# A state-space scan: where one of the sixteen input scalings of two state pairs is done

## The chip, the cores and the metric

The kernel runs on one core of one Trainium2 chip. Five engines work side by side, each through its own list of instructions in order: TensorE (matrix products and transposes, in the profile PE, with its weight loads as PEld), VectorE (DVE), ScalarE (ACT), GpSimd (POOL) and SyncE (SP), whose queue starts the DMA transfers. An instruction that needs what another engine makes waits for a semaphore, and everything behind it on its engine waits too.

The metric is the device time of one execution in microseconds (us), taken as the median of several runs.

## The reference

The input is 8 images of 64 x 64 pixels with 192 channels. Two residual layers follow each other. The first (convolutions, a chunked state-space layer, two projections) is not touched by the change. The second is a two-dimensional selective scan; cut to what matters here:

```python
xs = jnp.stack([x_flat, x_t], axis=1)                              # row order, column order
xs = jnp.concatenate([xs, jnp.flip(xs, axis=-1)], axis=1)          # and both backwards: K = 4 directions
x_dbl = jnp.einsum('bkdl,kcd->bkcl', xs, x_proj_weight)            # 12 for dt, 16 for B, 16 for C
delta = jax.nn.softplus(dts + dt_projs_bias[None, :, :, None])
A = -jnp.exp(A_logs).reshape(K, D_INNER, D_STATE)                  # D_INNER = 384, D_STATE = 16

def step(hst, inp):
    d, bm, cm, uu = inp
    dA = jnp.exp(d[..., None] * A[None])
    dBu = (d * uu)[..., None] * bm[:, :, None, :]
    hst = dA * hst + dBu
    y = jnp.einsum('bkdn,bkn->bkd', hst, cm)
    return (hst, y)
```

So for every direction, each of 384 channels and each of 16 states there is a recurrence over 4096 tokens. Its decay is exp(delta * A), its input is delta * u * B, and its output is multiplied by C and summed over the 16 states. The change concerns the product (delta * u) * B.

## The kernel before, in words

The program first computes layer 0 for all images, until about 4,900 us, and then goes image by image through layer 1. In layer 1 the function `scan` builds the work of an image. Its outer loop runs over *steps*: 4 directions k times 8 stretches c of 512 tokens, so 32 steps an image and 256 in all. In directions 2 and 3 the stretches and the scans run backwards. A step has 24 *units*: 8 pairs p of states, and for each pair 3 blocks d of 128 channels. A tile of a unit holds on its 128 partitions 2 states of 64 channels; the two halves f of the block lie beside each other.

What a unit needs, and the lines that make it:

- `weigh` (L1592, ScalarE) makes `pw`. Here tokens lie on the partitions, 4 groups j of 128, and a row has the 384 channels of delta * u (`duT`). For state i of pair p the row is multiplied by that token's B, one number per partition (`bt`). The result goes into every other run of 64 columns of `pw`, so that both states of a pair stand side by side. A pair needs 4 x 2 = 8 such scalings, two pairs sixteen. They serve all three units of the pair.
- `supply` (L1618, TensorE) turns `pw` by 8 transposes of 128 x 128 into `g` in PSUM: channels and states on the partitions, 512 tokens along the row.
- `decay` (L1607, ScalarE) makes `ea` = exp(delta * A) from `dr`, two instructions.
- `run` (L1634, VectorE) does the two scans `hs` = ea * state + g, starting from `cy`, the last state of the step before (a direction's first step starts from zero). GpSimd then copies the last column into `cy` (L1646) and multiplies `hs` by C into `hc` (L1648).
- `collect` (L1663, TensorE) sums the two states of `hc` into `y` in PSUM, over all pairs. In direction 0 and for p = 0 a product for the skip connection (L1661) stands ahead of it.
- `add` (L1672, L1674, VectorE) adds the finished `y` of the three blocks to `yacc`.

The order of all this is written out by hand in `main`; no planner changes it. Behind the scans of unit u are issued: `decay` of unit u + 2, then three, three or two `weigh` for d = 0, 1, 2 (they are taken from one list, `todo`, ten ahead), `supply` of unit u + 1, `collect` of unit u - 1, `add` of unit u - 2, and last the pieces that prepare the next step. Those pieces (`prepare`) stand at fixed units: the projection p_d on TensorE behind units 2, 3 and 4 (L1481), its copy `xdbl` on VectorE behind 5 (L1488), `bt` on VectorE behind 7 (L1504), p_dt on TensorE behind 7, 9 and 12 (L1510), the softplus on ScalarE behind 8, 10 and 13 (L1517, L1518), `de` on VectorE behind 9, 11 and 14 (L1523), its transpose p_du on TensorE behind 11, 14 and 16 (L1532), and `duT` on VectorE behind 12, 15 and 17 (L1539). Here a unit's number in its step is 3p + d, and a piece "behind" a unit stands in the lists after what `main` issues for that unit. All loads go through SP's queue.

Buffers: three of `ea`, three each of `hs` and `hc`, two of `g`, eight of `pw` (two pairs). `scan` is entered for each image after a stretch in which the image before is finished and the new one is prepared.

Of the kernel before, what the change touches and what calls it, by code (L numbers as in the profile page):

```python
# [9 lines left out]
AF = mybir.ActivationFunctionType  # L10
# [18 lines left out]
NB1 = TT // 128  # L29
# [1003 lines left out]
def layer1(tc, consts, x1s, mv1, out, w_in, w_x, w_dt, w_out):  # L1033
    nc = tc.nc
# [6 lines left out]
    with ExitStack() as ctx:  # L1041
# [49 lines left out]
        o = lambda ins: keeper[-1](ins)  # L1091
# [343 lines left out]
        def scan(xo):  # L1435
# [149 lines left out]
            def weigh(s, p, j, i):  # L1585

                st = state[s]
                if i == 0:
                    st["pw", p, j] = pools["pw1"].tile([128, 2 * DT, 2, 64], F32, name="pw")
                n = 2 * p + i  # L1590
                o(
                    nc.scalar.activation(  # L1592
                        st["pw", p, j][:, :, i],
                        st["duT"][:, j].rearrange("p (g c) -> p g c", c=64),
                        AF.Copy,
                        scale=st["bt"][:, j, n : n + 1],
                    )
                )

            def decay(u):  # L1600
                s, p, d = units[u]
# [79 lines left out]
            def prologue(f, mq, front_pools):  # L1681

                yield "wait", "front"
                front_pools.close()
                for name, n in (("pr1", 2), ("dr1", 4), ("pw1", 8), ("bc1", 3), ("e1", 3)):
                    spool(name, n)
                load_first = prepare(0, lambda name: mq.tile([128, TT], F32, name=name, tag="mm"))
                ready.update({fn.__name__: fn for at in sorted(load_first) for fn, *_ in load_first[at]})
                r = yield step("SP", 0.1, ready["load"])
                yield "take", "mm"  # L1690
                r += 3.5
                for d in range(DT):
                    r = yield step("PE", 0.95, lambda: ready["project"](d), r)
                r = yield step("DVE", 0.7, ready["keep"])
                f.give("mm", r)
                f.at["xd"] = r
                yield "take", "mm"
                yield step("PE", 0.6, ready["turn_b"])
                r = yield step("DVE", 0.2, ready["keep_b"])
                f.give("mm", r)  # L1700
                f.at["bt"] = r
                load_c(0, 0)
                for d in range(DT):
                    yield "wait", ("du", d)
                for t in todo[:10]:
                    yield step("ACT", 0.55, lambda: weigh(*t), f.free["ACT"])
                for u in range(2):
                    yield step("ACT", 1.35, lambda: decay(u), None, "explog")
# [19 lines left out]
            def main():  # L1728
                for name, n, kw in (("h1", 3, {}), ("y1", 1, dict(space=PSUM)), ("g1", 2, dict(space=PSUM))):
                    spool(name, n, **kw)  # L1730
                supply(0)
                rest = iter(todo[10:])
                nu = len(units)
                for u, (s, p, d) in enumerate(units):
                    if p == 0 and d == 0:
                        pieces = prepare(s + 1) if s + 1 < len(steps) else {}
                    s2, p2 = (s, p + 1) if p < NP1 - 1 else (s + 1, 0)
                    if s2 < len(steps) and d == 0:
                        load_c(s2, p2)
                    run(u)  # L1740
                    if u + 2 < nu:
                        decay(u + 2)
                    for _ in range((3, 3, 2)[d]):
                        if t := next(rest, None):
                            weigh(*t)
                    if u + 1 < nu:
                        supply(u + 1)
                    if u >= 1:
                        collect(u - 1)
                    if u >= 2:  # L1750
                        add(u - 2)
                    for f, *args in pieces.get(p * DT + d, ()):
                        f(*args)
                collect(nu - 1)
                add(nu - 2)
                add(nu - 1)
                cx.close()
# [136 lines left out]
```

## Time and profile before

| what | value |
|---|---|
| median of 3 runs | 23751.5 us (23744.67 to 23764.05) |
| the profiled execution | 23759.13 us, its span 23757.4 us |
| busy: PE, DVE, ACT, POOL | 21089.6, 21274.2, 21040.0, 16067.4 us |
| scalings `pw`, ScalarE, L1592 | 16384, mean 601 ns |
| decays `ea`, ScalarE, L1607 | 12288, mean 709 ns |
| scans `hs`, VectorE, L1634 | 10752 of mean 1262 ns and 1536 of 1202 ns |
| products `hc`, GpSimd, L1648 | 6144, mean 2375 ns |
| one ordinary step (9142.23 to 9207.80 us) | 65.57 us |

In a row of the groups, the line, the engine and the operation are followed by what is written and read, the number of instructions, their busy time and the mean of one. After the last bar stands the time that the engine was idle just before them, and what ended it. The durations of successive instructions of VectorE and ScalarE overlap by some tens of nanoseconds, so what an instruction costs its engine is rather the distance to the start of the next. In a timeline each row is a start, a duration, an instruction or several equal ones in a row, and in brackets the idle time before it with what ended that.

### The profile page before, as it was taken

To read this page: it belongs to the slowest core of one execution; us is meant where nothing else is said; L and a number is where in the kernel's file an instruction comes from. 1 tells how busy PE (TensorE), PEld (TensorE's weight loads), DVE (VectorE), ACT (ScalarE), POOL (GpSimd) and SP (SyncE) were. 2 spreads that over 40 slices of the span, in tenths; PEclk is the share of its full clock that TensorE was granted. 3 is DMA by queue.
4 is the path that set the end of the run, shared out by engine and by line. 5 is a ranking of instruction groups with operands and counts; after the bars stand their busy time and mean duration, and the time that the engine had idled before them with its cause. 6 is when DMAs were issued, how large, how long until landed. Compare 5 with 4: busy or idle time off the path is not lost.

```text
span 23757.4 us, 313126 instructions
## 1 busy us (share of the span) xinstructions
PE 21089.6 (89%) x100804; PEld 10279.5 (43%) x100804; DVE 21274.2 (90%) x22093; ACT 21040.0 (89%) x37507; POOL 16067.4 (68%) x12871
## 2 busy tenths in 40 slices
PE   7999999978888888888888888888888888888888
PEld 4444444434444444444444444444444444444444
DVE  7888888779998999899989998999899989998998
ACT  5666766669998999899989998999899989998998
POOL 1111111149995999599959985998699769976997
PEclk8999999989999999999999999999999999999999
DMA  2111111133233323333233233323332233233332
GB/s 50 45 44 44 46 44 43 39 99 81 81 79 107 81 82 78 107 81 82 76 112 81 82 77 109 81 81 79 110 82 81 78 107 82 81 85 100 82 83 67
DMA packets 1368290, 1859.75 MB, mean 78 GB/s; under 512 B 268576, under 2 KB 697024, under 8 KB 1357440
## 3 DMA queue, kind: packets, MB, share of 16 engines
q1 hardware_dynamic: 1366656, 1839.73, 28.7%
q8 instruction: 810, 13.27, 0.2%
q14 instruction: 824, 6.75, 0.1%
HBM read 1225.98 MB, written 210.50 MB: 60 GB/s over the span
## 4 chain that ended last, share of the span: by engine, by line
POOL 43%; PE 24%; ACT 15%; DVE 7%; issue 6%; DMA 4%; SPq 1%; POOLq 0%; ACTq 0%; DVEq 0%
POOL hc L1648 40%; ACT pw L1592 6%; ACT ea L1607 6%; POOL cy L1646 3%; PE p_f L956 3%; DMA xc<-xo 2%; DVE xs L1202 2%; PE p_f L976 2%; PE p_x L448 2%; PE y L1663 2%; PE p_o L873 2%; PE p_y L790 1%; PE g L1618 1%; PE p_d L1481 1%; PE p_z L531 1%
## 5 line engine op out<-in xcount | busy, mean ns | idle before, releaser
L1648 POOL TENSOR_TENSOR hc<-hs,cb 128x1024 f32<-128x1024 f32 x6144 | 14592.9, 2375 | 12.0 <-POOL cy L1646 9.9
L1634 DVE TENSOR_TENSOR_SCAN hs<-ea,cy,g 128x512 f32<-128x512 f32 x10752 | 13024.0, 1262 | 608.6 <-PE g L1618 411.1
L1592 ACT ACTIVATE pw<-duT,bt 128x384 f32<-128x384 f32 x16384 | 8874.1, 601 | 20.2 <-DVE duT L1539 20.2
L1607 ACT ACTIVATE ea<-dr,an 128x512 f32<-128x512 f32 x12288 | 8120.5, 709 | 189.2 <-DVE hs L1634 170.8
L1663 PE MATMUL y<-hc,sel 128*64 128x512 f32 x24576 | 6624.0, 617 | 1841.3 <-POOL hc L1648 1819.2
L1618 PEld LDWEIGHTS g<-ident,pw 128*128 128x128 f32 x49152 | 5288.7, 141 | 4336.8 <-issue 2671.4
L1618 PE MATMUL g<-ident,pw 128*128 128x128 f32 x49152 | 6788.4, 279 | 60.1 <-ACT pw L1592 28.6
L1646 POOL COPY cy<-hs 128x2 f32<-128x2 f32 x6144 | 1164.2, 189 | 3373.5 <-DMA out_x<-xl 1733.8
L1663 PEld LDWEIGHTS y<-hc,sel 128*64 128x64 f32 x24576 | 1225.9, 134 | 3254.1 <-POOL hc L1648 3031.3
L1634 DVE TENSOR_TENSOR_SCAN hs<-ea,g 128x512 f32<-128x512 f32 x1536 | 1763.7, 1202 | 159.0 <-PE g L1618 115.6
L365 POOL TENSOR_TENSOR s<-xs 96x512 f32<-96x512 f32 x64 | 121.1, 1892 | 2033.7 <-DVE xs L343 1522.9
L1202 DVE SCALAR_TENSOR_TENSOR xs<-pad,p,xs 128x4096 f32<-128x4096 f32 x192 | 860.9, 4484 | 43.4 <-ACT xs L1192 36.2
L1510 PE MATMUL p_dt<-xdbl,wd 13*128 13x512 f32 x1536 | 857.2, 639 | 41.0 <-DVE de L1523 39.1
L365 POOL TENSOR_TENSOR s<-sq 96x512 f32<-96x512 f32 x128 | 211.6, 1653 | 964.1 <-ACT sq L378 899.8
L1481 PE MATMUL p_d<-xc,wx 128*44 128x512 f32 x1536 | 791.6, 598 | 22.6 <-DMA xc<-xo 22.0
L343 DVE SCALAR_TENSOR_TENSOR x<-xx,p,x 96x512 f32<-96x512 f32 x1024 | 785.2, 815 | 19.4 <-ACT x L332 19.4
L956 PE MATMUL p_f<-h,wf 96*128 96x512 f32 x1536 | 761.9, 632 | 24.4 <-ACT zs L550 14.0
L343 DVE SCALAR_TENSOR_TENSOR xs<-xin,p,xs 96x512 f32<-96x512 f32 x1024 | 749.3, 767 | 4.6 <-ACT xs L332 4.6
L976 PE MATMUL p_f<-m,wf 128*96 128x512 f32 x1536 | 692.9, 601 | 0.0
L1532 PEld LDWEIGHTS p_du<-ident,de 128*128 128x128 f32 x3072 | 323.5, 141 | 610.2 <-DVE de L1523 405.8
L448 PE MATMUL p_x<-h,wi 96*128 96x512 f32 x1024 | 544.5, 664 | 12.3 <-ACT h L405 11.1
L365 POOL TENSOR_TENSOR s<-x 96x512 f32<-96x512 f32 x64 | 96.2, 1502 | 626.3 <-DVE x L343 477.2
(202 smaller groups left out, 19557.2 us busy)
## 6 DMA issues: line engine op xcount, KB each, us to landing
cb<-cd SPq DMA_DIRECT2D x4096, 128.0 KB
dr<-de SPq DMA_DIRECT2D x3072, 128.0 KB
xc<-xo SPq DMA_DIRECT2D x256, 768.0 KB
e<-csd SPq DMA_DIRECT2D x256, 384.0 KB
xl<-x SPq DMA_DIRECT2D x256, 384.0 KB
ut<-xo SPq DMA_DIRECT2D x128, 768.0 KB
ut<-xo SPq DMA_DIRECT2D x256, 384.0 KB
xo<-xs SPq DMA_DIRECT2D x48, 1024.0 KB
```

Source lines behind the costliest of these rows:

```text
L343: nc.vector.scalar_tensor_tensor(im(out[:, ct]), tap(ct, j), w[:, ct, j : j + 1], im(out[:, ct]), ALU.mult, ALU.add)
L956: nc.tensor.matmul(ps, wf1[:, ct, mt * 128 : mt * 128 + 128], h[:, ct], start=ct == 0, stop=ct == 1)
L976: nc.tensor.matmul(ps[:CP], wf2[:, kt, ct * CP : ct * CP + CP], m[:, kt], start=kt == 0, stop=kt == 5)
L1202: nc.vector.scalar_tensor_tensor(xs, tap(j), kw[:, d, j : j + 1], xs, ALU.mult, ALU.add)
L1481: nc.tensor.matmul(st["p_d"][:44], wx[:, d, k], st["xc"][:, d], start=d == 0, stop=d == DT - 1)
L1592: nc.scalar.activation(st["pw", p, j][:, :, i], st["duT"][:, j].rearrange("p (g c) -> p g c", c=64), AF.Copy, scale=st["bt"][:, j, n : n + 1],
L1607: nc.scalar.activation(ea[:, f], state[s]["dr", d][:, f], AF.Exp, scale=an[:, k, p, at : at + 1])
L1618: nc.tensor.transpose(g[:, f, j * 128 : j * 128 + 128], state[s]["pw", p, j][:, 2 * d + f].rearrange("p a b -> p (a b)"), ident,)
L1634: nc.vector.tensor_tensor_scan(rev(h[:, f]), rev(ea[:, f]), rev(g[:, f]), 0.0 if first(s) else state[s - 1]["cy"][:, p, d, f : f + 1], ALU ...
L1646: o(nc.gpsimd.tensor_copy(st["cy"][:, p, d], h[:, :, last]))
L1648: o(nc.gpsimd.tensor_mul(hc, h, bc(st["cb", p], 1, [128, 2, TT])))
L1663: o(nc.tensor.matmul(y[half[f]], sel, hc[:, f], start=p == 0 and k > 0, stop=p == NP1 - 1))
```

## The change

In every second pair (p odd), the eighth scaling (j = 3, i = 1) is issued to VectorE as a `tensor_scalar_mul`; the other fifteen of two pairs stay on ScalarE. It is issued at the same place in the program's text. In VectorE's list this is behind the second scan of a unit: the list `todo` runs ten ahead, so the scaling of pair p + 1 (odd) comes up in the unit with even p and d = 1, which is units 1, 7, 13 and 19 of a step. The transposes for the unit after the next are the first to read it.

```diff
                 n = 2 * p + i
-                o(
-                    nc.scalar.activation(
-                        st["pw", p, j][:, :, i],
-                        st["duT"][:, j].rearrange("p (g c) -> p g c", c=64),
-                        AF.Copy,
-                        scale=st["bt"][:, j, n : n + 1],
-                    )
-                )
+                dst, src = st["pw", p, j][:, :, i], st["duT"][:, j].rearrange("p (g c) -> p g c", c=64)
+                scale = st["bt"][:, j, n : n + 1]
+                if p % 2 and (j, i) == (NB1 - 1, 1):
+                    o(nc.vector.tensor_scalar_mul(dst, src, scale))
+                else:
+                    o(nc.scalar.activation(dst, src, AF.Copy, scale=scale))
```

## The prediction

> A step is one direction and one stretch of 512 tokens. It has 24 units, numbered here u = 3p + d (pair p = 0 to 7, column block d = 0 to 2). S(u), hc(u), y(u) and g(u) are unit u's two scans (VectorE, L1634), product with C (GpSimd, L1648), sum (TensorE, L1663) and transposed input (TensorE, L1618).
>
> **What bounds the kernel now.** First the page: engine shares, then the chain.
>
> ```profile
> PE 21089.6 (89%) x100804; PEld 10279.5 (43%) x100804; DVE 21274.2 (90%) x22093; ACT 21040.0 (89%) x37507; POOL 16067.4 (68%) x12871
> ...
> POOL 43%; PE 24%; ACT 15%; DVE 7%; issue 6%; DMA 4%; SPq 1%; POOLq 0%; ACTq 0%; DVEq 0%
> ...
> L1648 POOL TENSOR_TENSOR hc<-hs,cb 128x1024 f32<-128x1024 f32 x6144 | 14592.9, 2375 | 12.0 <-POOL cy L1646 9.9
> L1592 ACT ACTIVATE pw<-duT,bt 128x384 f32<-128x384 f32 x16384 | 8874.1, 601 | 20.2 <-DVE duT L1539 20.2
> ```
>
> ScalarE is about as busy as VectorE, yet the chain runs mostly through GpSimd and TensorE. Next one ordinary step, 9142.23 to 9207.80 us: busy time of PE, PEld, DVE, ACT and POOL after the step's 65.57 us.
>
> ```profile
> 9142.23:9207.80 65.57, 57.78 (x318) 28.49 (x316) 63.18 (x61) 65.36 (x119) 60.04 (x49) 1.00 0.33 84
> ```
>
> ScalarE has 0.2 us idle, VectorE 2.4. That looks like a ScalarE bound, so I followed the step's timelines for each VectorE wait. VectorE first (from unit 1 on), then GpSimd:
>
> ```profile
> 9139.29 2.44 DVE L1634 TENSOR_TENSOR_SCAN hs<-ea,cy,g 128x512 f32<-128x512 f32 x2
> 9141.65 0.66 DVE L1674 TENSOR_TENSOR yacc<-yacc,y 128x512 f32<-128x512 f32 x1
> ...
> 9150.41 2.45 DVE L1634 TENSOR_TENSOR_SCAN hs<-ea,cy,g 128x512 f32<-128x512 f32 x2 [0.50 <-PE g L1618]
> ...
> 9158.06 0.19 DVE L1504 COPY bt<-p_b 128x64 f32<-128x64 f32 x1
> ...
> 9161.75 2.45 DVE L1634 TENSOR_TENSOR_SCAN hs<-ea,cy,g 128x512 f32<-128x512 f32 x2 [1.14 <-PE g L1618]
> ...
> 9186.71 7.13 DVE L1634 TENSOR_TENSOR_SCAN hs<-ea,cy,g 128x512 f32<-128x512 f32 x6
> 9194.06 7.36 DVE L1634 TENSOR_TENSOR_SCAN hs<-ea,cy,g 128x512 f32<-128x512 f32 x6 [0.22 <-PE g L1618]
> ```
>
> ```profile
> 9141.80 0.19 POOL L1646 COPY cy<-hs 128x2 f32<-128x2 f32 x1 [0.39 <-DVE hs L1634]
> ...
> 9156.03 2.38 POOL L1648 TENSOR_TENSOR hc<-hs,cb 128x1024 f32<-128x1024 f32 x1
> 9158.35 0.19 POOL L1646 COPY cy<-hs 128x2 f32<-128x2 f32 x1
> ...
> 9189.39 2.38 POOL L1648 TENSOR_TENSOR hc<-hs,cb 128x1024 f32<-128x1024 f32 x1
> 9191.69 0.20 POOL L1646 COPY cy<-hs 128x2 f32<-128x2 f32 x1
> ```
>
> TensorE runs g(u+1), y(u-1), g(u+2), y(u) in that order, so S(u+3) needs g(u+3), which stands behind y(u), which needs hc(u). From the end of S(u) that is about 2.6 us to the end of hc, 1.05 for y, 1.05 for g, 0.2 to start: 5.0 us, plus 1 us where a projection (p_d, p_dt) stands between. S(9) shows it: S(6) ends at 9155.8, hc(6) at 9158.41, y(6) runs at 9158.46, p_dt 9159.47, g(9) 9160.52, S(9) at 9161.75; VectorE had 4.8 us of work in those 5.95 and idled 1.14. So each wait is explained without ScalarE, and the whole step closes the same way: S(0) to S(2) back to back; hc(2), y(2), p_d, g(5), S(5); S(6), hc(6), y(6), p_dt, g(9), S(9), S(10); hc(10), hc(11), y(11), p_dt, g(14), S(14); then VectorE without a break to S(18); hc(18), y(18), g(21), S(21); and five hc end to end, 2.45 us apart, pace S(21) to S(23). That ring is 65.57 us. ScalarE (65.36) merely fits in. In direction 0, where TensorE has six more products at p = 0, the step is 66.5 us, and the waits of one such step (7580 to 7645 us) show ScalarE itself waiting 1 us:
>
> ```profile
> ACT ea L1607 <- DVE hs L1634: 1.0, 1, 1.0
> ```
>
> Only a direction's first step (65.0 us, scans 1.12 us apart instead of 1.18) is paced by ScalarE near its end.
>
> **What the skill says.** "SBUF — State Buffer", section Who interferes with whom: a VectorE instruction in a two-port mode, or with two SBUF inputs, and a GpSimd instruction exclude each other; the first holds the port pair for its whole length. Today's scan-stage VectorE work never does that: scans, duT, de and yacc read one operand from PSUM. Layer 0 shows the exclusion (timelines of VectorE and GpSimd):
>
> ```profile
> 1380.02 1.30 DVE L761 TENSOR_TENSOR st<-st,dec 64x384 f32<-64x384 f32 x1
> 1379.64 1.27 POOL L365 TENSOR_TENSOR s<-x 96x512 f32<-96x512 f32 x1 [4.06 <-DVE x L343]
> 1380.85 0.53 POOL L436 COPY cin<-cin 128x12 f32<-128x12 f32 x1
> ```
>
> L761 (541 ns in the median) waited for the GpSimd sum, ended 0.41 us after it (384 elements streaming), and GpSimd's next instruction, 0.19 us elsewhere, waited for it: the waiting VectorE instruction went first. "VectorE: DVE Perf Modes", section on the perf-mode tier table: fp32 tensor_scalar within SBUF runs at 2×. The trace agrees (price below).
>
> **The change, part by part.** Per step, four scalings (p odd, j = 3, i = 1) move, 1024 in all.
> *ScalarE* loses 1024 starts 0.505 us apart (three take 1.52 us from start to start of what follows): 2.0 us a step, worth nothing in the ring, for it is not in it.
> *VectorE* gains 1024 tensor_scalar 128x384. Nearest rows:
>
> ```profile
> L237 DVE TENSOR_SCALAR wf<-wf,p 96x768 f32<-96x768 f32 x2 | 1.2, 610 | 4.7 <-PE p_fb L227 4.7
> L248 DVE TENSOR_SCALAR dsk<-ident,p 128x128 f32<-128x128 f32 x3 | 0.7, 270 | 0.0
> ```
>
> (610 - 270)/640 = 0.53 ns an element, two a cycle; at 384 that is 406 ns, and VectorE instructions overlap by 0.08 us (a 0.66 us yacc costs 0.58), so 0.33 us. At one a cycle: 0.6 us, 0.53 net, without exclusion. I take 0.33. Behind a running hc it ends 0.21 us (384 at 0.53) after it.
> *Order.* In the built order it stands directly behind the second scan of units 1, 7, 13 and 19, with no semaphore wait of its own; the fourth transpose of g(u+2) now waits for VectorE too. No DMA moves. Behind it queue yacc or bt and the next scan; GpSimd's cy and hc wait if it holds the ports.
> - *Unit 1*: GpSimd is idle (the 0.39), so it goes at once; it lies in the unbroken run S(0) to S(2): **+0.33**. In direction 0 the ring there is TensorE's (y, skip product, p_d end to end, S(4) and S(5) idle 0.60 and 1.29): **0**.
> - *Unit 7*: S(7) ends at 9158.14, hc(6) at 9158.41, so it waits 0.27 and runs 0.21; cover is the 1.14 us before S(9): **0**.
> - *Unit 13*: GpSimd idle; S(14) waited 0.18 for g(14) (four scans take 4.97, elsewhere 4.78), so 0.33 - 0.18 = **+0.15**.
> - *Unit 19*: S(19) ends at about 9191.5, hc(18) at 9191.77: 0.48 for VectorE against 0.22 cover at S(21); cy(19) and the five hc in a row move by 0.25: **+0.25**.
>
> So +0.73 in the 168 ordinary steps: 123 us; +0.40 in the 56 later steps of direction 0: 22 us. The 32 first steps: two groups of three units take 7.73 at ScalarE's pace, GpSimd's is 7.36, so about -0.7, less 0.33: **-0.4**, -12 us. Sum **+133 us**: 23,759.1 (span 23,757.4 and 1.7 around it) becomes 23,892. The median of the runs is 7.6 below the profiled one: 23,885.
>
> **Rivals.**
> 1. *ScalarE is the bound; faster.* For: 65.36 of 65.57 busy. Against: no scan of the step waits for ScalarE. If so, a step falls to what VectorE then needs, 63.18 + 1.32 = 64.5: -1.07 x 256 = -270, 23,480. It decides if VectorE's 2.4 idle us shrink when ScalarE is early.
> 2. *One element a cycle.* 0.53, 0, 0.35, 0.3 = 1.2 (168 steps) and 0.65 (56): +238, less 12: 23,977. For: the output has a stride between its runs of 64, which neither row has.
> 3. *The waiting scaling loses the ports to the next hc* at units 7 and 19: 2.4 us more each, 1.6 after unit 7's cover: +4 x 224 = about +1000, 24,750. Against: the 1380 us rows.
> 4. *Hidden.* The 1.4 us fit the 2.4 idle us if VectorE's lateness at units 1, 13 and 19 is caught up before the next wait: 23,750. Against: no idle time stands between S(0) and S(2).
> That the change doesn't happen is excluded by the built order.
>
> **How the numbers follow.** My case 0.52 (alone 23,835 to 23,940), rival 1 0.08, rival 2 0.16, rival 3 0.10 (partly lost ports lie between), rival 4 0.14. Dropping rival 1 and most of rival 3 leaves 23,730 to 24,100. What a measurement here can tell is about 0.2%, 48 us. Faster is rival 1: 0.08; within is rival 4: 0.14; slower is the rest: 0.78.
>
> **What would show it.** The new row: near 0.41 us on average, longer behind units 7 and 19. Ordinary step 66.3, direction 0 66.9, first steps 64.6. ScalarE idle about 2.5 us a step, waiting for hs. GpSimd's cy grows behind the scalings, hc does not. Wrong if scans wait for pw or ea before, if hc lengthens by whole microseconds, or if the row is near 0.6 us (rival 2) or 2 us (rival 3).

## The result

| | median | runs |
|---|---|---|
| before | 23757.8 us | 4 (23744.67 to 23767.62) |
| after | 23876.9 us | 4 (23864.2 to 23878.98) |

The ratio is 1.0051, 95% interval 1.0039 to 1.0063: slower by 119 us, where 133 were forecast (the sum of the steps; 23,885 for the median). The profiled execution took 23878.98 us, its span 23876.9, which is 119.5 more than the span before.

The change makes the file two lines shorter here, so L1634 is now L1632, L1618 is L1616, L1648 is L1646 and L1646 is L1644; in the kernels of the experiments a line can stand one or two off again. The decays are L1605, the scalings L1596 on ScalarE and L1594 on VectorE. The page of the changed kernel, with the lines that answer to those of before, and the row of `ea`:

```profile
PE 21014.3 (88%) x100804; PEld 10295.5 (43%) x100804; DVE 21645.8 (91%) x23117; ACT 20657.4 (87%) x36483; POOL 16193.5 (68%) x12871
...
POOL 36%; PE 25%; ACT 21%; DVE 6%; issue 5%; DMA 4%; SPq 2%; POOLq 0%; ACTq 0%; DVEq 0%
...
L1646 POOL TENSOR_TENSOR hc<-hs,cb 128x1024 f32<-128x1024 f32 x6144 | 14569.5, 2371 | 12.5 <-POOL cy L1644 11.5
...
L1605 ACT ACTIVATE ea<-dr,an 128x512 f32<-128x512 f32 x12288 | 8138.1, 710 | 645.7 <-DVE hs L1632 624.1
...
L1596 ACT ACTIVATE pw<-duT,bt 128x384 f32<-128x384 f32 x15360 | 8350.1, 601 | 21.8 <-DVE duT L1539 21.8
...
L1644 POOL COPY cy<-hs 128x2 f32<-128x2 f32 x6144 | 1269.5, 207 | 3359.5 <-DMA out_x<-xl 1745.4
```

Two of these rows in the kernel before:

```profile
L1607 ACT ACTIVATE ea<-dr,an 128x512 f32<-128x512 f32 x12288 | 8120.5, 709 | 189.2 <-DVE hs L1634 170.8
L1646 POOL COPY cy<-hs 128x2 f32<-128x2 f32 x6144 | 1164.2, 189 | 3373.5 <-DMA out_x<-xl 1733.8
```

The engines' busy times moved as the change says: ScalarE lost 383 us and VectorE gained 372. `hc` kept its length (2375 ns before). `cy` grew from 189 to 207 ns. ScalarE's waits for `hs`, in the row of `ea`, grew from 171 to 624 us. The share of ScalarE in the chain rose from 15 to 21% although it does less; the runs below show that this share is not a bound.

The new operation, from the groups with shapes kept apart:

```profile
L1594 DVE TENSOR_SCALAR pw<-duT,bt 128x384 f32<-128x384 f32 x1024 | 503.4, 492 | 0.0
```

The same ordinary step as in the prediction (9299.82 to 9366.08 us here), busy time of PE, PEld, DVE, ACT and POOL after the length, and ScalarE's waits in it:

```profile
9299.82:9366.08 66.26, 57.47 (x317) 28.51 (x318) 64.57 (x64) 63.88 (x115) 60.60 (x49) 1.00 0.32 80
```

```profile
ACT ea L1605 <- DVE hs L1632: 2.1, 4, 0.9
```

ScalarE is busy for 63.9 us of 66.3 and idle for 2.4, of which it waits 2.1 for scans: the time that it was given is spent waiting. VectorE's idle time in the step fell from 2.39 to 1.69 us, and the rest of the 1.39 us that it gained in work, 0.69 us, is what this step grew by.

The timeline of VectorE around units 19 (9282.86), 1 (9298.92) and 7 (9315.66), then GpSimd's:

```profile
9278.16 4.79 DVE L1632 TENSOR_TENSOR_SCAN hs<-ea,cy,g 128x512 f32<-128x512 f32 x4
9282.86 0.57 DVE L1594 TENSOR_SCALAR pw<-duT,bt 128x384 f32<-128x384 f32 x1
9283.35 9.77 DVE L1632 TENSOR_TENSOR_SCAN hs<-ea,cy,g 128x512 f32<-128x512 f32 x8
...
9298.92 0.40 DVE L1594 TENSOR_SCALAR pw<-duT,bt 128x384 f32<-128x384 f32 x1
9299.23 0.68 DVE L1672 TENSOR_TENSOR yacc<-yacc,y 128x512 f32<-128x512 f32 x1
...
9315.66 0.56 DVE L1594 TENSOR_SCALAR pw<-duT,bt 128x384 f32<-128x384 f32 x1
9316.13 0.21 DVE L1504 COPY bt<-p_b 128x64 f32<-128x64 f32 x1
```

```profile
9280.84 2.37 POOL L1646 TENSOR_TENSOR hc<-hs,cb 128x1024 f32<-128x1024 f32 x1
9283.16 0.31 POOL L1644 COPY cy<-hs 128x2 f32<-128x2 f32 x1
9283.43 2.37 POOL L1646 TENSOR_TENSOR hc<-hs,cb 128x1024 f32<-128x1024 f32 x1
...
9299.07 0.29 POOL L1644 COPY cy<-hs 128x2 f32<-128x2 f32 x1 [0.39 <-DVE hs L1632]
...
9313.62 2.37 POOL L1646 TENSOR_TENSOR hc<-hs,cb 128x1024 f32<-128x1024 f32 x1
9315.94 0.32 POOL L1644 COPY cy<-hs 128x2 f32<-128x2 f32 x1
```

Behind unit 1, where GpSimd is idle, the scaling takes 0.40 us, and the next instruction starts 0.31 us after it. Behind units 19 and 7 an `hc` is running. There the scaling ends 0.22 and 0.23 us after that `hc` (9283.43 against 9283.21, 9316.22 against 9315.99), and `cy` behind it takes 0.3 us in place of 0.19. In all 1024, the medians by place are 396 ns (unit 1), 559 (unit 7), 396 (unit 13) and 569 (unit 19), and 535 of them came up while an `hc` was running: all ended before the next `hc` began, 0.22 us (median) behind the running one. GpSimd is held up at the other two places as well: `cy` takes 0.29 us behind units 1 and 13, and the `hc` after it starts 0.25 us after `cy` does, in place of 0.14.

Where the time went is seen best when a step is cut where its waits end. The table has the distances between the starts of scans, from the trace, in us (0-2 is from the start of S(0) to the start of S(2), 18-0 from S(18) to S(0) of the next step): the median over 160 ordinary steps (the last step of each image is left out, since what follows it is no step).

| from S to S | 0-2 | 2-6 | 6-9 | 9-13 | 13-15 | 15-18 | 18-0 | step |
|---|---|---|---|---|---|---|---|---|
| before | 5.88 | 11.12 | 8.39 | 11.26 | 5.47 | 8.23 | 15.21 | 65.56 |
| after | 6.21 | 11.12 | 8.39 | 11.26 | 5.61 | 8.23 | 15.45 | 66.26 |
| more | 0.33 | 0 | 0 | 0 | 0.14 | 0 | 0.24 | 0.70 |

The three stretches that grew hold units 1, 13 and 19; unit 7, in 6-9, cost nothing. A later step of direction 0 grew by 0.33 (66.51 to 66.84), a direction's first step shrank by 0.52 (0.32 in direction 0). With these, 160 x 0.70 + 56 x 0.33 - 24 x 0.52 - 8 x 0.32 = 115 us of the 119.5. These are medians; the 248 steps themselves, summed, grew by 110 us.

### The profile page after: what moved, and what is told of

Its sections match the earlier page's. It is cut to its first block, busy times and chain, and to the rows that moved or that the text cites. A ratio compares the mean times of both kernels' runs of the same rounds, so it can differ in the third digit from the quotient of the medians.

```text
span 23876.9 us, 313903 instructions
## 1 busy us (share of the span) xinstructions
PE 21014.3 (88%) x100804; PEld 10295.5 (43%) x100804; DVE 21645.8 (91%) x23117; ACT 20657.4 (87%) x36483; POOL 16193.5 (68%) x12871
## 4 chain that ended last, share of the span: by engine, by line
POOL 36%; PE 25%; ACT 21%; DVE 6%; issue 5%; DMA 4%; SPq 2%; POOLq 0%; ACTq 0%; DVEq 0%
POOL hc L1646 33%; ACT pw L1596 9%; ACT ea L1605 8%; POOL cy L1644 3%; PE p_f L956 3%; PE y L1661 3%; DVE xs L1202 2%; PE p_f L976 2%; PE p_x L448 2%; PE g L1616 2%; PE p_o L873 2%; PE p_y L790 1%; DMA xc<-xo 1%; DMA dr<-de 1%; PE p_z L531 1%
## 5 line engine op out<-in xcount | busy, mean ns | idle before, releaser
L1646 POOL TENSOR_TENSOR hc<-hs,cb 128x1024 f32<-128x1024 f32 x6144 | 14569.5, 2371 | 12.5 <-POOL cy L1644 11.5
L1632 DVE TENSOR_TENSOR_SCAN hs<-ea,cy,g 128x512 f32<-128x512 f32 x10752 | 13017.5, 1262 | 404.5 <-PE g L1616 180.7
L1605 ACT ACTIVATE ea<-dr,an 128x512 f32<-128x512 f32 x12288 | 8138.1, 710 | 645.7 <-DVE hs L1632 624.1
L1596 ACT ACTIVATE pw<-duT,bt 128x384 f32<-128x384 f32 x15360 | 8350.1, 601 | 21.8 <-DVE duT L1539 21.8
L1616 PEld LDWEIGHTS g<-ident,pw 128*128 128x128 f32 x49152 | 5299.9, 141 | 4165.9 <-issue 2487.8
L1616 PE MATMUL g<-ident,pw 128*128 128x128 f32 x49152 | 6673.6, 279 | 17.6 <-DVE hs L1632 12.5
L1644 POOL COPY cy<-hs 128x2 f32<-128x2 f32 x6144 | 1269.5, 207 | 3359.5 <-DMA out_x<-xl 1745.4
L1632 DVE TENSOR_TENSOR_SCAN hs<-ea,g 128x512 f32<-128x512 f32 x1536 | 1769.1, 1202 | 103.9 <-PE g L1616 48.0
```

The lines of the kernel that those rows point to most:

```text
L1596: o(nc.scalar.activation(dst, src, AF.Copy, scale=scale))
L1605: nc.scalar.activation(ea[:, f], state[s]["dr", d][:, f], AF.Exp, scale=an[:, k, p, at : at + 1])
L1616: nc.tensor.transpose(g[:, f, j * 128 : j * 128 + 128], state[s]["pw", p, j][:, 2 * d + f].rearrange("p a b -> p (a b)"), ident,)
L1632: nc.vector.tensor_tensor_scan(rev(h[:, f]), rev(ea[:, f]), rev(g[:, f]), 0.0 if first(s) else state[s - 1]["cy"][:, p, d, f : f + 1], ALU ...
L1644: o(nc.gpsimd.tensor_copy(st["cy"][:, p, d], h[:, :, last]))
L1646: o(nc.gpsimd.tensor_mul(hc, h, bc(st["cb", p], 1, [128, 2, TT])))
```

## The experiments

The question was which of the two halves of the change costs, which of its four places, how much of it is the exclusion between VectorE and GpSimd, and whether ScalarE's gain can be had where the waits are moved.

### Each half alone

First, ScalarE's relief alone:

```diff
                 if p % 2 and (j, i) == (NB1 - 1, 1):
-                    o(nc.vector.tensor_scalar_mul(dst, src, scale))
+                    pass
...
-                                state[s]["pw", p, j][:, 2 * d + f].rearrange("p a b -> p (a b)"),
+                                state[s]["pw", p, min(j, NB1 - 2) if p % 2 else j][:, 2 * d + f].rearrange("p a b -> p (a b)"),
```

> The four scalings of a step are left out altogether (TensorE's transposes read the neighbouring block j = 2 in their place, so that share of the output is another): ScalarE is relieved exactly as by the change, VectorE gets nothing. My theory, that the step is set by a ring through VectorE, GpSimd and TensorE and not by ScalarE: ordinary step 65.56 us as before, direction 0 66.5 as before, only a direction's first step shorter, by about 0.8 us; time about 23,730 us, ratio 0.999. Rival, that ScalarE sets the step (65.36 of 65.57 us busy): the step loses between 1.1 and 2.0 us, time 23,250 to 23,480 us, ratio 0.979 to 0.989.

Then VectorE's work alone, with all sixteen scalings on ScalarE and VectorE's result put into a tile that nothing reads:

```diff
+                o(nc.scalar.activation(dst, src, AF.Copy, scale=scale))
                 if p % 2 and (j, i) == (NB1 - 1, 1):
-                    o(nc.vector.tensor_scalar_mul(dst, src, scale))
-                else:
-                    o(nc.scalar.activation(dst, src, AF.Copy, scale=scale))
+                    o(nc.vector.tensor_scalar_mul(junk, src, scale))
```

> ScalarE keeps all sixteen scalings; VectorE does the four extra ones a step at the same places into a scratch tile that nobody reads. My theory: the cost is VectorE's part alone, so ordinary step 66.26 us and direction 0 66.84 as in the changed kernel; first steps a little longer than before, since ScalarE isn't relieved; time about 23,890 us, ratio 1.006. Rival, that ScalarE's relief pays for part of VectorE's work in the changed kernel: slower than the changed kernel by up to 2 us a step, up to 24,380 us, ratio 1.026.

The relief alone gave 23686.2 us, ratio 0.9980 (0.9972 to 0.9988); VectorE's work alone 23885.4 us, 1.0063 (1.0048 to 1.0078); the kernel before took 23741.3 us on that chip. An ordinary step of the relief run, by windows, and ScalarE's waits in it:

```profile
8178.52:8244.06 65.54, 57.39 (x318) 28.52 (x316) 63.17 (x60) 63.74 (x115) 59.94 (x49) 1.00 0.31 79
```

```profile
ACT ea L1605 <- DVE hs L1632: 1.5, 3, 0.6
```

For pairs with odd p the transposes read the block j = 2 in place of j = 3 here, so TensorE waits for an earlier scaling: if anything, this kernel has less to wait for than the changed one. ScalarE is busy 1.6 us less than before, and the step has the same length: the median of all ordinary steps is 65.56 us, unchanged to 0.01 in the whole step and in each of the seven stretches. So ScalarE, at 65.36 us busy of 65.57, was not what set the pace, and rival 1 falls. The gain of the run lies in other steps: 0.16 us in direction 0, 0.92 in the first steps of the other directions and 0.67 in direction 0's (56 x 0.16 + 24 x 0.92 + 8 x 0.67 = 36 us, and 41 when the steps themselves are summed; the measured gain is 55, its interval 28 to 66). That is more than the 27 us expected: the first steps gain more, and direction 0 gains where nothing was expected.

The second run has an ordinary step of 66.26 us: 0.33, 0.14 and 0.24 more in the same three stretches, and 0 in the others. Its row is that of the changed kernel:

```profile
L1596 DVE TENSOR_SCALAR junk<-duT,bt 128x384 f32<-128x384 f32 x1024 | 505.9, 494 | 0.0
```

So in the ordinary steps the whole loss is made by VectorE's part; ScalarE's part neither adds to it nor takes from it. The output here has no stride, and the row is the same.

### Each place alone

The condition was narrowed to one pair, so that only the scaling behind unit 1 (p = 1), unit 7 (p = 3) or unit 19 (p = 7) is VectorE's:

```diff
-                if p % 2 and (j, i) == (NB1 - 1, 1):
+                if p == 3 and (j, i) == (NB1 - 1, 1):
```

> Only the scaling behind unit 1 goes to VectorE, the other three of a step stay on ScalarE. My theory: ordinary step +0.33 us, direction 0 none (TensorE's products cover it): ordinary 65.89, time about +50 us, 23,810 us. Rival, that the cost follows VectorE's time alone: a quarter of the whole, +0.18 us a step.

> Only the scaling behind unit 7 goes to VectorE. My theory: it waits for the running hc but is covered by the 1.14 us wait ahead of S(9): step unchanged (65.56), time 23,755 us within 10. Rival, a quarter of the whole: +0.18 us a step, +30 us.

> Only the scaling behind unit 19 goes to VectorE. My theory: it waits for hc(18) and then holds back cy(19) and five hc in a row: +0.24 us a step, ordinary 65.80 and direction 0 66.75, its row near 0.57 us, time about +50 us. Rival, a quarter of the whole: +0.18 us in ordinary steps and +0.08 in direction 0.

Each ran once beside one run of the kernel before (23742.7 us):

| scaling of VectorE behind | time | ordinary step, more | stretch that grew | later step of direction 0, more |
|---|---|---|---|---|
| unit 1 | 23791.1 us | 0.32 | 0-2 | -0.06 |
| unit 7 | 23706.3 us | 0 | none | -0.16 |
| unit 19 | 23764.6 us | 0.24 | 18-0 | 0.08 |

A single run says little about a few tens of us: the time before the first scan of layer 1, which none of these edits touches, runs from 5031 to 5083 us in the traces of this case. The steps, which are medians over 160, say it clearly. In an ordinary step each place costs what it costs in the full change, and the fourth, unit 13, which was not run alone, is left with 0.70 - 0.32 - 0.24 = 0.14, which is what its stretch grew by. Unit 7 alone, from the groups and from VectorE's timeline:

```profile
L1594 DVE TENSOR_SCALAR pw<-duT,bt 128x384 f32<-128x384 f32 x256 | 148.1, 579 | 0.0
```

```profile
8198.85 0.56 DVE L1594 TENSOR_SCALAR pw<-duT,bt 128x384 f32<-128x384 f32 x1
...
8202.54 2.45 DVE L1632 TENSOR_TENSOR_SCAN hs<-ea,cy,g 128x512 f32<-128x512 f32 x2 [0.64 <-PE g L1616]
```

It is the longest of the four, because `hc` is running, and it is free: the idle time before S(9), 1.14 us in the kernel before, is 0.64 here, and S(9) starts when `g` is there, as it did. With ScalarE relieved of that one scaling, this kernel is even a little faster than the one before: its 248 steps, summed, are 16 us shorter, by the steps of direction 0 (-0.16 us) and the first steps of the others (-0.34). In direction 0, unit 1 costs nothing either, as the prediction said of its ring (the closed chain of waits that sets the length of a step), which is TensorE's there: the stretch 0-2 grows by 0.33 us and 2-6 shrinks by 0.38.

### The exclusion of the ports

An operation of VectorE that takes as long but does not exclude GpSimd, at the same four places, would tell the length of the new work from the exclusion. A sum along the row was tried, into the tile that nothing reads, with all scalings on ScalarE; whether it excludes GpSimd is seen in the lengths of `cy`. Two sizes were run, 192 elements and 256:

```diff
-                    o(nc.vector.tensor_scalar_mul(dst, src, scale))
+                    o(nc.vector.reduce_sum(junk[:, 0, :1], st["duT"][:, j, :256], axis=mybir.AxisListType.X))
```

> ScalarE keeps all scalings; VectorE does a sum over 192 elements[...] at the four places, into a scratch tile, in place of the scaling of 384. If it costs about the 0.31 us of the scaling without excluding GpSimd: its row the same at all four places, cy back to 189 ns, +0.33, 0, +0.14 and only +0.1 behind unit 19: ordinary step 66.1 us against 66.26. Rival, that the longer rows behind units 7 and 19 and the 0.24 us of unit 19 have nothing to do with GpSimd: longer rows there again and 66.26 us.

> As the run with the sum over 192 elements, with 256, so that VectorE's instruction is as long as the scaling (its row near 396 ns): +0.33 behind unit 1, +0.14 behind unit 13, as the scaling. Behind unit 19 without the exclusion of GpSimd 0.33 - 0.22 = 0.1 us at most and perhaps none, with it (rival) 0.24; the row the same at all four places.

The sum of 192 took 321 to 331 ns, the sum of 256 took 385 to 394 at all four places, against 396 for the scaling where nothing hinders it. The latter, from the groups and from the timelines of VectorE and GpSimd at unit 19:

```profile
L1596 DVE TENSOR_REDUCE junk<-duT 128x1 f32<-128x256 f32 x1024 | 401.6, 392 | 0.0
```

```profile
8289.11 4.79 DVE L1632 TENSOR_TENSOR_SCAN hs<-ea,cy,g 128x512 f32<-128x512 f32 x4
8293.82 0.39 DVE L1596 TENSOR_REDUCE junk<-duT 128x1 f32<-128x256 f32 x1
8294.13 9.76 DVE L1632 TENSOR_TENSOR_SCAN hs<-ea,cy,g 128x512 f32<-128x512 f32 x8
```

```profile
8291.80 2.37 POOL L1646 TENSOR_TENSOR hc<-hs,cb 128x1024 f32<-128x1024 f32 x1
8294.11 0.19 POOL L1644 COPY cy<-hs 128x2 f32<-128x2 f32 x1
```

Here `hc` is running too (8291.80 to 8294.17), and yet VectorE starts the next scan after 0.31 us, and `cy` keeps 0.19, here and at the other three places. So what stretched the scaling from 0.40 to 0.57 us and `cy` from 0.19 to 0.31 is the exclusion, which "SBUF — State Buffer" in the Trainium skill, section Who interferes with whom, describes for two-port modes; these traces agree.

| per ordinary step, more | unit 1 | unit 7 | unit 13 | unit 19 | step |
|---|---|---|---|---|---|
| scaling (the change) | 0.33 | 0 | 0.14 | 0.24 | 0.70 |
| sum of 256, same length | 0.33 | 0 | 0.14 | 0.07 | 0.53 |
| sum of 192, shorter | 0.26 | 0 | 0.07 | 0.00 | 0.33 |

The exclusion is 0.17 us of the step's 0.70, all of it behind unit 19; the rest is plain time in VectorE's list. That `cy` is 0.1 us longer behind units 1 and 13, and the `hc` after it as much later, costs nothing: the sum, which leaves them alone, costs as much there. The lower rows also show the cover: from 0.33 us of work unit 1 pays all, unit 13 pays 0.14 and unit 19 pays 0.07. With 0.07 us less work each of the three pays 0.07 less. The kernel with the sum of 192 took 23810.2 us in one run (before: 23742.7), that with the sum of 256 took 23866.1 (before: 23762.5).

### Another order around it

Can ScalarE's gain be had in ordinary steps too, if the parts of the ring that TensorE makes are shortened? The projections p_d and the first p_dt stand on TensorE between `y` and the next `g`. In the next two kernels they are issued one place later, behind the next `g`; the copy `xdbl` then has to stand behind unit 6. One has all scalings on ScalarE, the other has the change:

```diff
-                    5: [(keep,)],
-                    6: [(turn_b,)],
+                    6: [(keep,), (turn_b,)],
...
                     if u + 1 < nu:
                         supply(u + 1)
+                    for f, *args in late:
+                        f(*args)
+                    late = []
...
                     for f, *args in pieces.get(p * DT + d, ()):
-                        f(*args)
+                        if p * DT + d < 8 and f.__name__ in ("project", "step"):
+                            late.append((f, *args))
+                        else:
+                            f(*args)
```

> The kernel before, with p_d of units 2, 3, 4 and the first p_dt put one place later in TensorE's list, behind the next unit's transposes and ahead of the next sum y (the copy xdbl moves from unit 5 to 6 with them). If these products stand in the ring between y(u) and g(u+3), VectorE's waits of 0.43, 0.50 and 1.14 us at S(4), S(5) and S(9) shrink to some 0.3 together; ring about 63.9 us, and now ScalarE's 65.36 us sets the ordinary step: -0.2 us; direction 0 about -0.9 us; time about 23,670 us, ratio 0.996. Rival, that those waits come from ScalarE or from GpSimd alone: no change, ratio 1.000.

> The changed kernel with the same move of p_d and the first p_dt as in the run before this one. My theory: with the ring shortened to about 63.9 us, the scalings on VectorE add some 1.0 (unit 7 has less cover), 64.9 us, and ScalarE needs only 63.3: 0.65 us under the ordinary step of before and 0.45 under that of the same order without the change; time about 23,590 us, ratio 0.993 to before, and here the scaling on VectorE is a gain. Rival, that VectorE's extra work costs its 0.7 us whatever the order: slower than the same order without the change by 0.5%, ratio 1.001.

| | time | ratio to before | 0-2 | 2-6 | 6-9 | 9-13 | 13-15 | 15-18 | 18-0 | step |
|---|---|---|---|---|---|---|---|---|---|---|
| order, all on ScalarE | 23695.3 | 0.9981 (0.9974 to 0.9988) | 0 | -0.94 | -0.60 | 0.74 | 0.45 | 0 | 0.06 | -0.28 |
| order, with the change | 23714.0 | 0.9988 (0.9979 to 0.9996) | 0.33 | -0.94 | -0.28 | 0.63 | 0.14 | 0 | 0.24 | 0.12 |

The two waits that were aimed at did shrink: with all scalings on ScalarE 1.54 us were won up to S(9). But most of it came back behind that. The later p_dt makes the softplus and `de` late, as VectorE's timeline of the first of the two shows:

```profile
9156.53 2.45 DVE L1633 TENSOR_TENSOR_SCAN hs<-ea,cy,g 128x512 f32<-128x512 f32 x2 [0.64 <-PE g L1617]
...
9167.85 0.69 DVE L1523 SCALAR_TENSOR_TENSOR de<-spa,p_dt 128x512 f32<-128x512 f32 x1 [0.45 <-ACT spa L1518]
```

For the kernel with the change a step of 64.9 us was expected, and it was 65.68: a miss. With all on ScalarE the step came out as expected (-0.28 for -0.2), but direction 0 gained 0.10 us where 0.9 was expected. So in the last three kernels only p_d was moved (`f.__name__ == "project"` in the diff), with all scalings on ScalarE, with the change, and with VectorE doing only the scalings behind units 7 and 13:

```diff
-                if p % 2 and (j, i) == (NB1 - 1, 1):
+                if p in (3, 5) and (j, i) == (NB1 - 1, 1):
```

> The kernel before with only p_d of units 2, 3, 4 one place later in TensorE's list (and xdbl behind unit 6, where the wait ahead of S(9) covers it); the first p_dt stays where it was. My theory: the ring loses the 0.94 us that it lost between S(2) and S(6) in both runs with the moved order and gives nothing back later, 64.6 us; ScalarE's 65.36 us then sets the ordinary step: about -0.2 us; direction 0 about -0.9; time ratio 0.996. Rival, that the later p_d delays xdbl, bt and p_dt and is given back behind S(9) as before: 65.3 us or more, ratio 0.998 or above.

> The changed kernel, all four scalings on VectorE, with p_d one place later. My theory: ring 64.6 + 0.7 = 65.3 us, ScalarE 63.3: ordinary step 65.3 us, as long as that of the same order without the change; the change is then worth nothing in ordinary steps and something in first steps; ratio 0.996. Rival, that the change costs its 0.7 us in any order: 66.0 us, ratio 0.999 or above.

> p_d one place later, and only the scalings behind units 7 and 13 on VectorE, the two that cost the ring 0 and 0.14 us. My theory: ring 64.6 + 0.14 = 64.76 us, ScalarE 65.36 - 1.0 = 64.35: ordinary step 64.8 us, below both the kernel before and the changed one; direction 0 about 65.6; time ratio about 0.992. Rival, that ScalarE's relief is worth nothing in any order: 65.4 us, ratio 0.997.

| p_d later | time | ratio to before | 0-2 | 2-6 | 6-9 | 9-13 | 13-15 | 15-18 | 18-0 | step |
|---|---|---|---|---|---|---|---|---|---|---|
| all on ScalarE | 23664.2 | 0.9958 (0.9943 to 0.9972) | 0 | -0.94 | 0.02 | 0.07 | 0.45 | 0 | 0.06 | -0.32 |
| with the change | 23718.9 | 0.9981 (0.9973 to 0.9989) | 0.33 | -0.94 | 0.02 | 0.34 | 0.14 | 0 | 0.24 | 0.13 |
| units 7 and 13 only | 23602.3 | 0.9932 (0.9917 to 0.9947) | 0 | -0.94 | 0.02 | 0.34 | 0.14 | 0 | 0 | -0.44 |

One ordinary step with all scalings on ScalarE, by windows, with a VectorE instruction and a TensorE instruction of it:

```profile
8198.88:8264.11 65.23, 58.45 (x318) 28.44 (x318) 63.24 (x61) 65.14 (x119) 59.92 (x49) 1.00 0.33 85
```

```profile
8240.01 0.69 DVE L1523 SCALAR_TENSOR_TENSOR de<-spa,p_dt 128x512 f32<-128x512 f32 x1 [0.43 <-ACT spa L1518]
```

```profile
8238.89 0.77 PE L1617 MATMUL g<-ident,pw 128*128 128x128 f32 x5 [0.41 <-ACT pw L1591]
```

This looks like the step before, with ScalarE busy for nearly the whole of it and waiting for nobody. The difference is that VectorE and TensorE now wait for ScalarE's results. By these waits ScalarE sets the pace here. Scalings taken from it bear this out in two stretches: 13-15 goes from +0.45 to +0.14, which is what the scaling behind unit 13 costs VectorE, and 18-0 from +0.06 to 0 with units 7 and 13 moved. ScalarE's relief alone was not run in this order. With two scalings a step taken from it:

```profile
8189.18:8254.31 65.13, 57.35 (x318) 28.53 (x316) 63.75 (x62) 64.39 (x117) 60.17 (x49) 1.00 0.32 83
```

```profile
8207.62 0.66 DVE L1488 COPY xdbl<-p_d 44x512 f32<-44x512 f32 x1
...
8210.56 0.38 DVE L1593 TENSOR_SCALAR pw<-duT,bt 128x384 f32<-128x384 f32 x1
...
8213.64 2.45 DVE L1631 TENSOR_TENSOR_SCAN hs<-ea,cy,g 128x512 f32<-128x512 f32 x2 [0.21 <-PE g L1615]
...
8219.36 2.45 DVE L1631 TENSOR_TENSOR_SCAN hs<-ea,cy,g 128x512 f32<-128x512 f32 x2 [0.33 <-POOL cy L1643]
```

```profile
8216.08 1.08 PE L1660 MATMUL y<-hc,sel 128*64 128x512 f32 x4 [0.54 <-POOL hc L1645]
```

It is the fastest kernel of the case: 0.9932 of the kernel before, against 0.9958 for the same order with all on ScalarE. Its ordinary step, expected at 64.8 us, took 65.12. The rows tell why: `xdbl` now stands between S(6) and S(7) and has used up most of VectorE's idle time there. S(8) starts 5.75 us after S(6) (8205.25 and 8211.00 us); it is 5.43 us in this order without the scaling, and 5.32 in the changed kernel of the old order, where the scaling was free. So S(8) and its `hc` are late, `y` waits 0.54 us for `hc`, and S(11), behind them through p_dt and `g`, waits 0.33. (The row names `cy`, but no scan reads that `cy` in this step; S(11) starts 0.14 us after the end of `g`, in the median.) The place that was free before the order changed is free no longer. The loss is in the medians of both kernels that have this scaling: S(11) starts 5.70 us after S(9), and 5.37 without it. The way it takes, through `hc`, `y` and p_dt, is read from one step and was not tested by a run of its own.

Where the 62 us between 23664.2 and 23602.3 come from is told by the steps: -0.12 in 160 ordinary ones (-19 us), +0.16 in 56 of direction 0 (+9), but -1.63 in 24 first steps (65.23 to 63.60, -39 us) and -0.52 in 8 (-4), which makes -53, and -44 when the steps themselves are summed. It is mostly in the first steps that ScalarE's relief pays. With all four scalings on VectorE the same order lost 55 us (23718.9), and its ordinary step was 65.69 us where 65.3 was expected, another miss: those behind units 1 and 19 cost 0.33 and 0.24 in each ordinary step, as in the old order.

## Why the prediction was right, point by point

- **What bounds the step.** The prediction read a ring through scans, `hc`, `y`, p_d or p_dt and `g`, in which ScalarE has no part. The relief run shows it: 1.6 us less of ScalarE's work changed an ordinary step by 0.00. One row of the changed kernel's step seems to speak against it: the idle time before S(5), 0.73 us, is put down to `pw`. But a scan doesn't read `pw`; three scalings happened to end at 9307.90, next to the end of g(5) at 9307.86, and S(5) started at 9308.00. So it is in all 160 ordinary steps: 113 us of the scans' idle time are put down to `pw` before S(5), and yet S(5) starts 0.14 us after the end of g(5) in the median, as it does in the kernel before and as S(4) and S(9) do after theirs. The stretch 2-6 is 11.12 us with and without the relief.
- **ScalarE's relief is worth nothing there and comes back as waiting.** 2.1 us of waits for `hs` in the step shown, about 2.5 us of idle time forecast, 2.4 measured in all.
- **The price of the operation.** 406 ns were forecast from two rows of other shapes, 396 were measured; 0.33 us in VectorE's list forecast, 0.31 to 0.33 measured. Rival 2 rested on the stride of the output. The traces agree with the 2× that "VectorE: DVE Perf Modes" in the Trainium skill gives for 32-bit `tensor_scalar` within SBUF in its section on the perf-mode tier table, with the stride too: the rows behind the forecast give 0.53 ns an element, and the two sums along the row about 1.0, (392 - 327)/64.
- **Behind a running `hc`.** The end 0.21 us after it was forecast; 0.22 and 0.23 us were seen. The waiting instruction of VectorE went ahead of the next `hc` in all 535 cases, so rival 3 falls, and `cy` grew behind all four scalings while `hc` did not. (The 0.19 us that the prediction gives for the GpSimd copy of layer 0 is its shortest; its median is 0.53.)
- **The four places.** Forecast +0.33, 0, +0.15, +0.25; measured +0.33, 0, +0.14, +0.24. In direction 0 unit 1 was forecast to cost nothing; alone it came to -0.06.
- **The steps.** 66.3, 66.9 and 64.6 us were forecast for an ordinary step, a later one of direction 0 and a first step; 66.26, 66.84 and 64.52 were measured (66.16 for the eight first steps of direction 0, which the forecast didn't tell apart). Rival 4, that it is hidden, falls with the first of these.

What was less exact: the relief was counted as nothing in direction 0, where alone it gives 0.16 us a step, 9 us in all. In the first steps -0.4 was the sum of -0.7 and 0.33. Relief alone gives -0.92 there, and the change -0.52, so VectorE's part comes to +0.40: both terms were too small, and their errors cancel in part, which is luck. VectorE's work alone costs only 0.10 in these steps. The stretches show where the two halves fail to add: the changed kernel has the relief's gains in 13-15 and 15-18 (-0.25 and -0.18), and VectorE's cost in 0-2 (0.33) on top, while VectorE's work alone gets 0.16 of its cost back in 13-15. It looks as if VectorE's part costs its full price once ScalarE no longer sets the pace; no run tests that, and it is worth 24 x 0.30 = 7 us.

The prediction's 5.0 us from the end of S(u) to S(u+3) is 4.9 by its own terms; with 1.05 for p_dt that is the 5.95 of S(9). The sum of 133 stood 14 us above the result: an ordinary step grew by 0.70 and not 0.73 (168 x 0.03 = 5 us), a later one of direction 0 by 0.33 and not 0.40 (56 x 0.07 = 4 us), and the first steps gave 3 us more. That leaves 121, and the span grew by 119.5. (All this is reckoned with medians.)

## What to carry to other kernels

An engine that is busy for 99.7% of a step need not be what sets its length: follow each wait of the step to what released it, and if the engine is in none of them, relief of it is worth nothing there, as in the ordinary steps here (0.00 of 1.6 us). In other stretches of the same kernel it can pay: the first steps of the directions gained 0.92 us. Work that is moved to another engine is paid by place: the same scaling cost 0.33, 0, 0.14 and 0.24 us, by how much idle time stood between it and the next wait. One of four places moved alone, the free one, made the kernel no slower; all four made it 119 us slower. And idle time can be spent once: when the copy `xdbl` was moved into the 1.14 us before S(9), the scaling that had been free there was not free any more.

## What the runs showed of the hardware

- A VectorE scaling of 128x384 in 32 bits that comes up while a GpSimd product is running waits for its end, goes ahead of GpSimd's next product (in all 535 cases of the changed kernel), and ends 0.22 us after the running one; GpSimd's copy that comes up meanwhile takes 0.31 us in place of 0.19. Where GpSimd is idle, the scaling takes 0.40 us and still makes the copy 0.29. That the handover is so cheap, 0.17 us on the path in 0.70, was the least certain term.
- A sum along 256 elements on VectorE took 392 ns and one along 192 took 327, so about one element a nanosecond, and both ran beside GpSimd's product without any sign of hindrance on either engine.
- The output's stride (runs of 64 elements, every other one) cost VectorE's scaling nothing: mean 492 ns with it, 494 without.
